# Layer 0's q, k and v from 15 block products in place of 18, in a fused two-layer attention kernel

## The chip, the cores and the metric

The kernel runs on one core of one Trainium2 chip. A core has five engines that work side by side, each through its own queue, strictly in the order in which its instructions were compiled: TensorE (PE: matrix products into PSUM), VectorE (DVE), ScalarE (ACT: activations and copies), GpSimd (POOL) and SyncE (SP, used here to issue DMA transfers). They wait for each other through semaphores. The metric is the device time of one execution in microseconds (us), smaller is better. PSUM has eight banks of 128 x 512 float32; a product of TensorE goes to one of them and has to be copied or used from there before the bank can be taken again.

## The reference, cut to what matters

The input x is 8 images of 32 x 32 positions (T = 1024) with 384 channels, float32. Layer 0 is attention with 6 heads of 64 and decomposed relative positions, after a group norm; layer 1 is causal attention with one head of 384 and, for images 0 to 4, an FFN of two products with sign-binarised weights whose results are scaled by the group's absolute maximum and clipped. Of layer 0 this is what the change concerns:

```python
qkv = x.reshape(b, hw, c) @ qkv_w + qkv_b        # (1024 x 384) @ (384 x 1152), per image
qkv = qkv.reshape(b, hw, 3, NH, HD).transpose(2, 0, 3, 1, 4)
```

In blocks of 128 channels, q transposed (3 blocks of output channels x 1024 positions) is a 3x3 block matrix of weights times a 3x2 block matrix of the image (3 blocks of channels, 2 halves of 512 positions). The plain way takes 3 x 3 x 2 = 18 block products for q, as many for k and for v.

## The kernel before, in words

The images go one after the other in the order 5, 0, 1, 2, 3, 4, 6, 7. For each: layer 0's q, k, v, the position terms, the scores and the output projection (`layer0`, `attend0_fast`), then layer 1 (`attention1`), then for images 0 to 4 the FFN (`ffn`). The group norm of the next image is made during layer 1 of the present one. A second, general path of the program stands behind a branch that this input doesn't take; the names in the profile have f_ in front of the fast path's tiles.

*q, k (L438, L466, L468).* `project_qk(b, xT, m)` makes one block of 128 output channels for both halves: three products each of 128x128x512 accumulate in a PSUM bank. m = 0 to 2 is q, 3 to 5 is k. A float32 product is two passes of TensorE, so q and k take 72 passes of 512 columns per image. ScalarE brings the first half out (with scale and bias), VectorE the second. k is stored in a permuted order of positions.

*Position terms (L484, L489, L490).* Behind the block that follows q block p, `positions(p)` multiplies q block p by the relative position table (tile rel; called rel(p) below): for each half two products in two banks. ScalarE copies one half of the rows of each bank out, VectorE the other, into the two pages called far. SP writes them to DRAM and reads them back skewed into near. `place(p, ...)` then rounds near to its high part (ScalarE, L517, twice 64x1024) and its low part (VectorE, L519), and SP and GpSimd copy these into r (L524, eight transfers each per p). The scores (L588, q times k, with L592, r times a unit pattern added into the same bank) need r.

*v (L536, L538, L539).* `values(j)` makes 128 positions x 384 channels from three products whose stationary operand is the image (every second position, `keys`) and whose moving operand is the weight, 384 columns: 8 x 3 x 2 = 48 passes. ScalarE and VectorE copy out in turn.

*Ahead of time.* Where the present image has an FFN, two blocks of the next image's q are made inside it: m = 0 between the two halves of the FFN's layer norm (`ffn`, behind the last transpose) and m = 1 between the FFN's first product y1 (L898) and its second y2 (L939). Their PSUM banks stay taken until layer 0.

*The FFN's other work.* Between y1 and y2 stand VectorE's maximum (L909, L852), GpSimd's all-reduce over partitions (L854), and the Gelus of `activate` (ScalarE L924, L925, VectorE L926), which make each block of activations as a high part hi and a low part lo. After y2 comes another maximum and all-reduce, then GpSimd clips y2 in eight pieces (L949) and VectorE adds them to x (L953), whose result GpSimd sends out (L994). These last steps (`finish`, `add`, kept in `unfinished`) are called inside the next image's layer 0, behind `positions(2)`.

The tile framework orders each engine's instructions ahead of time from its own estimates, within the order of the program and of `issue_after`, and puts in the semaphores; on the chip each engine keeps to that order. Buffers come from pools: image (11 buffers of 3 x 1024), flat (larger), page (1024 wide), small, and o_tile, the PSUM banks.

Of the kernel before, what the change touches and what calls it, by code (L numbers as in the profile page):

```python
# [37 lines left out]


# [3 lines left out]
class Pools:  # L43
    def __init__(self, ctx, tc, path):
# [5 lines left out]
        self.image_ = pool("image", 11)  # L50
# [25 lines left out]
def conv_attn_hybrid(  # L76
# [35 lines left out]
    wqkv_sb, wproj_sb, wv_sb = (tile_of(n, [P, NC, w]) for n, w in (("wqkv_sb", 3 * C), ("wproj_sb", C), ("wv_sb", C)))  # L112
    bqk, bv, b1_sb = (tile_of(n, [P, w]) for n, w in (("bqk", 6), ("bv", NC), ("b1_sb", NM)))
# [5 lines left out]
    def load_weights(pools):  # L119
# [8 lines left out]
        src = qkv_w.rearrange("(p k) o -> p k o", k=NC)  # L128
        for i in range(3):
            nc.sync.dma_start(out=wqkv_sb[:, :, ts(i, C)], in_=src[:, :, ts(i, C)])  # L130
# [5 lines left out]
        nc.scalar.mul(bqk[:, 0:NPAIR], bqk[:, 0:NPAIR], qscale)  # L136
        nc.scalar.mul(rel, rel, 1.0 / qscale)
        early = pools.small.tile([P, 1], F32, tag="early", name="early_root")
        nc.scalar.activation(early, ones[:, 0:1], AF.Sqrt)

# [70 lines left out]
    w2s = store.tile([P, NM * C], F32R, name="w2s")  # L211
    wqk = const.tile([P, NC, C], F32, name="wqk")
# [92 lines left out]
    def stages(pools):  # L305
# [125 lines left out]
        ahead = {}  # L431
# [11 lines left out]
        def layer0(b, xT):  # L443
# [5 lines left out]
            r = []  # L449
# [3 lines left out]
            def queries_keys(m):  # L453
                p = m % NPAIR
                bias = bqk[:, m : m + 1]
                made = ahead.pop((b, m)) if (b, m) in ahead else project_qk(b, xT, m)
                for half, ps in enumerate(made):
# [16 lines left out]
            def positions(p):  # L474

                if p < 1:
                    *pages, near = (pools.page(f"{n}_{b}_{p}") for n in ("far0", "far1", "near"))
                else:
                    room = pools.flat(f"far_{b}_{p}")
                    *pages, near = (room[:, ts(i, T)] for i in range(3))  # L480
                for half in range(2):
                    ps = [pools.o_tile(f"rel_{b}_{p}_{half}_{par}") for par in range(2)]
                    for par in range(2):
                        nc.tensor.matmul(  # L484
                            ps[par], rel[rows[par]].rearrange("d a n -> d (a n)"), q[rows[par], p, ts(half, 512)],
                            start=True, stop=True,
                        )
# [19 lines left out]
            def place(p, near, pages, behind=(None, None)):  # L507
# [12 lines left out]
                for part in range(4):  # L520
                    for d in range(2):
                        for i in range(2):
                            half = part % 2 if d else part // 2
                            (nc.gpsimd if i else nc.sync).dma_start(  # L524
                                out=r[part][:, p, :].bitcast(F32).rearrange("(m i) t -> i m t", i=4)[2 * i + d],
# [14 lines left out]

            near = []
            for m in range(2 * NPAIR):
                queries_keys(m)
                if 0 < m <= NPAIR:
                    near.append(positions(m - 1))
                if m == NPAIR and unfinished:
                    unfinished.pop()()

                    early = pools.small.tile([P, 1], F32, tag="early", name=f"early0_{b}")
                    nc.scalar.activation(early, k[:, 0, T - 1 :], AF.Exp, scale=0.0)  # L550
            for j in range(NJ):
                values(j)
            r.extend(pools.image(f"r_{b}_{part}", F32R) for part in range(4))
# [18 lines left out]
        def attend0_fast(residual, b, q, k, r, v, later):  # L572
# [10 lines left out]
            def scores(p, c, half):  # L583

                sc = [pools.o_tile(f"s0_{b}_{p}_{c}_{half}_{par}") for par in range(2)]
                with behind_last():
# [4 lines left out]
                    for par in range(2):  # L591
                        last_matmul[0] = nc.tensor.matmul(  # L592
                            sc[par], unit[rows[par], c // 2 % 2].rearrange("i h w -> i (h w)"),
                            r[2 * (c // 4) + c % 2][rows[par], p, ts(half, 512)], start=False, stop=True,
# [81 lines left out]
        def attend0_general(residual, b, q, k, r, v, later):  # L676
# [3 lines left out]
            def scores(u):  # L680
# [6 lines left out]
                for half in range(2):  # L687
# [3 lines left out]
                    for i in range(4):  # L691
                        nc.tensor.matmul(
                            sc[half][:, ts(i, P)], r[2 * half + i % 2][rows, p, ts(j, P)],
# [179 lines left out]
        def ffn(xt, b, gn):  # L873

            xs = [pools.halves(f"{n}_{b}", F32R) for n in ("lnT_2", "lnlo_2")]
            for half in range(2):
# [4 lines left out]
                if half == 0 and gn is not None and pools.fast:  # L881
                    with tc.issue_after(last_transpose[0]):
                        ahead[AFTER[b], 0] = project_qk(AFTER[b], gn, 0)

            early = pools.small.tile([P, 1], F32, tag="early", name=f"early_{b}")
# [27 lines left out]
            if gn is not None and pools.fast:  # L913
                ahead[AFTER[b], 1] = project_qk(AFTER[b], gn, 1)
# [3 lines left out]
            def activate(j, m0, m1):  # L918
# [131 lines left out]
```

## Time and profile before

| | us |
|---|---|
| median of 3 runs | 2351.95 (2351.21 to 2352.78) |
| the profiled execution | 2350.82 |
| its span in the profile | 2348.8 |
| TensorE busy | 2324.9 (99%), granted clock 0.999 |
| VectorE, ScalarE, GpSimd busy | 1433.9, 1041.7, 316.6 |
| q and k products (L438), 576 passes | 257.4 busy |
| v products (L536), 384 passes | 125.2 busy |
| image 1's layer 0, end of y2 to the first score | 595.36 to 637.78 |

How to read it: busy time is the sum of an engine's instructions in the execution; the share is of the span. In a table by stages each row gives a stretch, its length, then the busy time and the number of instructions of PE, PEld, DVE, ACT and POOL, the granted TensorE clock, the busy share of the DMA engines and their GB/s. PEld is TensorE's loading of its stationary operand, which overlaps its products. In a row of a group, the numbers behind the bar are its busy time and the mean of one instruction in ns, then the idle time of the engine just before it and what ended it. In rows of one line, durations are minimum/median/maximum in ns with the first and last start in us. The end of a matmul is modelled, some 0.16 us after the next one starts; the time that one takes from the stream is the distance of starts.

### The profile page before, as it was taken

What the parts mean: (1) busy time and instruction counts of PE and PEld (TensorE: products, weight loads), DVE (VectorE), ACT (ScalarE), POOL (GpSimd) and SP (SyncE); (2) the same over time, 40 slices, a digit from 0 to 9 for tenths busy, and PEclk for the clock granted to TensorE, in tenths of its full rate; (3) what the DMA queues carried; (4) which work ended last, traced back from release to release, by engine and by line L of the source; (5) the groups of instructions that cost most, each with busy time, mean ns of one, the idle gap of its engine ahead of it and who ended that gap; (6) DMA issues with size and microseconds to landing.
All of it is one profiled execution on the core that took longest, in us unless ns stands there. A gap on an engine that the chain in (4) does not pass through costs nothing.

```text
span 2348.8 us, 26174 instructions
## 1 busy us (share of the span) xinstructions
PE 2324.9 (99%) x9442; PEld 1288.2 (55%) x9442; DVE 1433.9 (61%) x2302; ACT 1041.7 (44%) x1763; POOL 316.6 (13%) x421
## 2 busy tenths in 40 slices
PE   7999999999999999999999999999999999999998
PEld 3445544568545577445684455864457744554454
DVE  3685568665587347684466864558734668525851
ACT  3551156137463256642365522747324656115621
POOL 0420013000230001310002300023000131001300
PEclk9999999999999999999999999999999999999999
DMA  6431361130631003520107211063101262017100
GB/s 166 146 117 37 104 146 38 54 135 1 144 99 68 20 21 91 118 88 14 41 12 166 65 68 41 1 138 105 68 1 41 68 139 63 1 51 146 45 1 29
DMA packets 154795, 169.99 MB, mean 72 GB/s; under 512 B 113408, under 2 KB 126048, under 8 KB 153120
## 3 DMA queue, kind: packets, MB, share of 16 engines
q1 hardware_dynamic: 134416, 98.93, 17.2%
q0 software_dynamic: 17184, 69.22, 9.7%
q8 instruction: 77, 1.26, 0.2%
q10 hardware_dynamic: 3056, 0.08, 0.1%
q14 instruction: 62, 0.51, 0.1%
HBM read 75.38 MB, written 42.47 MB: 50 GB/s over the span
## 4 chain that ended last, share of the span: by engine, by line
PE 99%; DVE 1%; DMA 0%; issue 0%; ACT 0%; DVEq 0%
PE f_s L588 14%; PE f_av L613 14%; PE f_qk L438 11%; PE f_s L775 8%; PE f_av L790 8%; PE f_y L939 7%; PE f_y L898 7%; PE f_pj L386 5%; PE f_v L386 5%; PE f_v L536 5%; PE f_q L734 5%; PE f_s L592 4%; PE f_rel L484 2%; PE f_pt L314 1%; PE f_den L631 0%; DMA f_gnT<-in_xT 0%
## 5 line engine op out<-in xcount | busy, mean ns | idle before, releaser
L598 ACT ACTIVATE f_pr<-f_s 128x512 f32<-128x512 f32 x768 | 413.6, 595 | 54.2 <-PE f_s L592 46.8
L588 PE MATMUL f_s<-f_q,f_k 64*128 64x512 f32 x1536 | 399.0, 595 | 0.0
L605 DVE TENSOR_TENSOR f_sum<-f_sum,f_pr 128x1024 f32<-128x1024 f32 x288 | 365.8, 1270 | 22.6 <-ACT f_pr L598 0.5
L613 PE MATMUL f_av<-f_pr,f_v 128*64 128x512 f32 x1536 | 339.4, 594 | 0.0
L592 PE MATMUL f_s<-f_r,unit 64*128 64x512 f32 x768 | 307.6, 792 | 0.0
L438 PE MATMUL f_qk<-f_gnT,wqkv_sb 128*128 128x512 f32 x576 | 257.4, 600 | 1.5 <-DVE f_gnT L349 1.5
L588 PEld LDWEIGHTS f_s<-f_q,f_k 64*128 64x128 f32 x1536 | 145.7, 186 | 127.4 <-issue 67.3
L613 PEld LDWEIGHTS f_av<-f_pr,f_v 128*64 128x64 f32 x1536 | 106.2, 137 | 196.3 <-issue 192.4
L775 PE MATMUL f_s<-f_q,f_lnT 128*128 128x512 f32 (+3 forms) x576 | 195.9, 488 | 0.0
L790 PE MATMUL f_av<-f_v,f_pr 128*128 128x385 f32 x576 | 195.3, 486 | 0.0
L438 PEld LDWEIGHTS f_qk<-f_gnT,wqkv_sb 128*128 128x128 f32 x576 | 108.0, 191 | 143.2 <-issue 131.5
L784 ACT ACTIVATE f_pr<-f_s 128x512 f32<-128x512 f32 (+3 forms) x96 | 47.1, 491 | 267.7 <-DVE f_s L780 220.7
L524 POOL DMA_DIRECT2D f_r<-f_far x192 | 102.2, 535 | 461.7 <-DVE f_far L519 450.9
L790 PEld LDWEIGHTS f_av<-f_v,f_pr 128*128 128x128 f32 x576 | 108.2, 190 | 77.3 <-issue 11.5
L775 PEld LDWEIGHTS f_s<-f_q,f_lnT 128*128 128x128 f32 x576 | 102.0, 190 | 77.8 <-issue 53.8
L902 ACT ACTIVATE f_h<-f_y,b_sb 128x256 f32<-128x256 f32 x240 | 100.9, 472 | 67.5 <-PE f_y L898 66.9
L909 DVE TENSOR_REDUCE am<-f_h 128x1 f32<-128x1024 f32 (+2 forms) x80 | 71.5, 946 | 96.3 <-ACT f_h L902 96.3
L734 PE MATMUL f_q<-f_lnT,wqk 128*128 128x512 f32 x288 | 127.5, 592 | 0.0
L386 PE MATMUL f_pj<-wproj_sb,f_oT 128*128 128x384 f32 x384 | 127.3, 488 | 0.0
L386 PE MATMUL f_v<-wv_sb,f_lnT 128*128 128x384 f32 x384 | 126.5, 486 | 0.0
L536 PE MATMUL f_v<-wqkv_sb,f_gnT 128*128 128x384 f32 x384 | 125.2, 486 | 0.0
L592 PEld LDWEIGHTS f_s<-f_r,unit 64*128 64x128 f32 x768 | 75.1, 187 | 90.0 <-issue 90.0
(153 smaller groups left out, 3024.9 us busy)
## 6 DMA issues: line engine op xcount, KB each, us to landing
f_far<-f_far SPq DMA_DIRECT2D x48, 512.0 KB, 3.2
f_r<-f_far POOLq DMA_DIRECT2D x192, 128.0 KB, 3.9
f_r<-f_far SPq DMA_DIRECT2D x192, 128.0 KB, 3.2
f_gnT<-in_xT SPq DMA_DIRECT2D x24, 512.0 KB, 4.6
f_x<-in_x SPq DMA_DIRECT2D x32, 384.0 KB, 7.5
out_y<-f_x POOLq DMA_DIRECT2D x28, 384.0 KB, 4.4
f_far<-f_far SPq DMA_DIRECT2D x128, 64.0 KB, 4.9
f_w1a<-w1s POOLq DMA_DIRECT2D x5, 1536.0 KB, 7.0
```

Source lines behind the costliest of these rows:

```text
L386: nc.tensor.matmul(ps[:, :C], xT[:, k, ts(j, P)], w[:, k, cols], start=(k == 0), stop=(k == NC - 1))
L438: nc.tensor.matmul(made[half], wqkv_sb[:, i, ts(m, P)], xT[:, i, ts(half, 512)], start=(i == 0), stop=(i == NC - 1))
L536: nc.tensor.matmul(ps, keys[:, i, j // 2, j % 2], wqkv_sb[:, i, 2 * C :], start=(i == 0), stop=(i == NC - 1))
L588: nc.tensor.matmul(sc[par], k[rows[par], p, ts(c, P)], q[rows[par], p, ts(half, 512)], start=True, stop=False)
L592: last_matmul[0] = nc.tensor.matmul(sc[par], unit[rows[par], c // 2 % 2].rearrange("i h w -> i (h w)"), r[2 * (c // 4) + c % 2][rows[par], ...
L598: last_exp[0] = nc.scalar.activation(pr[:, ts(par, 512)], sc[par], AF.Exp).ins
L605: adds.append(nc.vector.tensor_tensor(total, total, pr, ALU.add).ins)
L613: last_matmul[0] = nc.tensor.matmul(av[ts(par, HD), :], v[:, c, ts(2 * p + par, HD)], pr[:, ts(par, 512)], start=(c == 0), stop=(c == NJ - 1),
L734: nc.tensor.matmul(ps, wqk[:, k, ts(m, P)], xT[:, half, k, :], start=(k == 0), stop=(k == NC - 1))
L775: nc.tensor.matmul(sc[:, lo:], xT[:, c // 4, k, ts(c % 4, P)], q[:, half, k, lo:], start=(k == 0), stop=(k == NC - 1),)
L790: nc.tensor.matmul(av[:, : C + 1], prs[c][:, ts(j - c, P)], v[:, c, :], start=(c == 0), stop=(c == j))
L898: nc.tensor.matmul(ps, w1k[i // 2][:, ts(m, P)], xs[i % 2][:, half, i // 2, :], start=(i == 0), stop=(i == 2 * NC - 1))
```

## The change

q, k and v (three sets) are each made from 15 products in place of 18. A product is a sum of weight blocks times a sum of image blocks. The six blocks of a result are sums of the products in groups, so that the products are collected in six PSUM banks, A to F. B and A collect eleven of them as running sums: after most of their products ScalarE copies the bank's present value out (`keep`), and the next product goes on in the same bank. Four times per set GpSimd subtracts one such copy from another; at the end VectorE brings each bank out, adding or subtracting a kept sum (`put_queries`, `put_keys`, `put_values`). Below, "A5" is product number 5 in bank A; "n6", "m7" are names of kept sums.

- The weight sums (`weight_forms`) are made once at the start: GpSimd for q, VectorE for k and v. For v the products are 4 x (128 x 128 x 128): the moving operand is a weight block of 128 columns.
- The image sums (`image_forms`), eleven operations of 128x512, are made by VectorE for image 5 and by GpSimd, during the layer 1 before, for the others.
- Ahead of time, six q products are made in the layer-norm gap, five between y1 and y2, and the twelfth (B3) is issued within y2; three are left to layer 0. k's products are laid around the three `positions(p)`, two before each, and `finish` is called behind `positions(0)`; TensorE's order of all these is fixed (`in_turn`). The Exp table's early load moves behind k.
- Memory: one image buffer less (10); r takes three flats shared by pairs of p; far and near of p = 0 and the FFN's hi and lo move to flats; the FFN writes x to DRAM in the layer norm and reads it back during y2 (`spilt`, `xagain`).

```diff
+PROD_ORDER = (
+    ("A", 5, "m5"), ("B", 11, "m11"), ("A", 13, "n0"), ("B", 6, "n1"), ("A", 12, "n2"), ("B", 0, "n4"),
+    ("A", 4, "n3"), ("B", 1, "n5"), ("A", 10, "n6"), ("D", 8, None), ("C", 7, "m7"),
+    ("B", 3, None), ("F", 9, None), ("A", 2, None), ("E", 14, None),
+)
+PROD_FIRST = tuple(PROD_ORDER[i] for i in (9, 12, 14, 0, 1, 2, 3, 4, 5, 6, 7, 8, 10, 11, 13))
+PROD_COMBINE = {"n1": ("n0", "n1"), "n2": ("n2", "m11"), "m7": ("m7", "n3"), "n6": ("n5", "n6")}
...
+    def weight_forms(pools, eng, raw, s):
+        add(s1, w(0, 1), w(0, 2))
+        add(f(8), w(0, 0), s1)
+        add(s2, w(2, 0), w(2, 2))
+        add(f(9), w(2, 1), s2)
...
+        def image_forms(b, xT, eng):
+            sub(5, x(2, 1), x(0, 1))
+            sub(5, f[5], x(1, 1))
+            add(2, x(2, 0), x(2, 1))
+            sub(0, f[2], x(1, 0))
+            sub(1, x(1, 1), f[0])
+            add(11, f[1], x(0, 1))
+            sub(4, x(0, 0), f[2])
+            add(7, f[4], x(0, 1))
+            add(13, f[7], x(1, 1))
+            sub(6, x(1, 0), x(2, 0))
+            sub(12, x(2, 0), x(0, 0))
...
+            def multiply(self, ps, r, start):
+                x, w = self.forms[r], wf[:, r, self.s, :]
+                if self.s < 2:
+                    in_turn(ps, w, x, start=start, stop=True, skip_group_check=True)
+                    return
+                keys = x.rearrange("p (g i n) -> p g n i", g=2, n=2)
+                for j in range(4):
+                    in_turn(
+                        ps[:, ts(j, P)], keys[:, j // 2, j % 2], w, start=start and j == 0, stop=True, skip_group_check=True
+                    )
+            def keep(self, ps, name):
+                dst = self.kept(name)
+                if self.s == 2:
+                    nc.scalar.copy(dst, ps)
+                    return
...
+                nc.scalar.activation(dst, ps, AF.Identity, bias=bias, scale=scale)
+            def run(self, n, final=None):
+                for self.now in range(self.at, self.at + n):
+                    bank, r, name = self.order[self.now]
...
+                    self.multiply(self.banks[bank], r, start)
+                    if name is not None:
+                        self.keep(self.banks[bank], name)
+                    if name in PROD_COMBINE:
+                        dst, other = PROD_COMBINE[name]
+                        nc.gpsimd.tensor_tensor(self.part[dst], self.part[dst], self.part[other], ALU.subtract)
...
-                if p < 1:
-                    *pages, near = (pools.page(f"{n}_{b}_{p}") for n in ("far0", "far1", "near"))
-                else:
-                    room = pools.flat(f"far_{b}_{p}")
-                    *pages, near = (room[:, ts(i, T)] for i in range(3))
+                room = pools.flat(f"far_{b}_{p}")
+                *pages, near = (room[:, ts(i, T)] for i in range(3))
...
+            def put_queries(ps, kept, p, half, op):
+                nc.vector.scalar_tensor_tensor(q[:, p, ts(half, 512)], ps, qscale, kept, ALU.mult, op)
+            def put_keys(ps, kept, p, half, op):
+                dst = k[:, p, ts(half, 512)].rearrange("d (g n i) -> d g i n", n=2, i=P)
+                ps, kept = (t.rearrange("d (g i n) -> d g i n", n=2, i=P) for t in (ps, kept))
+                nc.vector.tensor_tensor(dst, ps, kept, op)
+            def put_values(ps, kept, p, half, op):
+                ps, kept = (t.rearrange("t (j c) -> t j c", j=4) for t in (ps, kept))
+                nc.vector.tensor_tensor(v[:, 4 * half : 4 * half + 4, ts(p, P)], ps, kept, op)
+            def products():
+                forms = xf.pop(b)
+                of_q = ahead.pop(b, None) or ProductSet(b, 0, forms, PROD_FIRST)
+                of_q.run(N_PROD - of_q.at, put_queries)
+                of_k, of_v = (ProductSet(b, s, forms) for s in (1, 2))
+                for p in range(NPAIR):
+                    of_k.run(2, put_keys)
+                    near.append(positions(p))
+                    if p == 0 and unfinished:
+                        unfinished.pop()()
+                of_k.run(N_PROD - of_k.at)
+                early = pools.small.tile([P, 1], F32, tag="early", name=f"early0_{b}")
+                nc.scalar.activation(early, k[:, 0, T - 1 :], AF.Exp, scale=0.0)
+                of_v.run(N_PROD, put_values)
...
-                        ahead[AFTER[b], 0] = project_qk(AFTER[b], gn, 0)
+                    ahead[AFTER[b]] = ProductSet(AFTER[b], 0, xf[AFTER[b]])
+                    last_product[0] = last_transpose[0]
+                    ahead[AFTER[b]].run(6)
+            nc.sync.dma_start(out=spilt, in_=xt.rearrange("p j c -> p (j c)"))
...
-                ahead[AFTER[b], 1] = project_qk(AFTER[b], gn, 1)
+                ahead[AFTER[b]].run(5)
...
+                room = pools.flat(f"hilo_{b}_{j}", F32R)[:, : 3 * T].rearrange("p (i m q) -> p i m q", i=2, q=P)
...
+                if j == 4:
+                    xt = pools.flat(f"xagain_{b}")[:, : NJ * C].rearrange("p (j c) -> p j c", j=NJ)
+                    nc.sync.dma_start(out=xt.rearrange("p j c -> p (j c)"), in_=spilt)
...
+                raw = load_weights(pools)
+                weight_forms(pools, nc.gpsimd, raw[0], 0)
...
+                xf[ORDER[0]] = image_forms(ORDER[0], gn, nc.vector)
+                weight_forms(pools, nc.vector, raw[1], 1)
+                weight_forms(pools, nc.vector, raw[2], 2)
...
+                            xf[AFTER[b]] = image_forms(AFTER[b], made, nc.gpsimd)
```

## The prediction

> **What bounds the kernel now.** I read the busy shares and the chain that ended last first, then the groups that the change touches.
>
> ```profile
> PE 2324.9 (99%) x9442; PEld 1288.2 (55%) x9442; DVE 1433.9 (61%) x2302; ACT 1041.7 (44%) x1763; POOL 316.6 (13%) x421
> PE 99%; DVE 1%; DMA 0%; issue 0%; ACT 0%; DVEq 0%
> L438 PE MATMUL f_qk<-f_gnT,wqkv_sb 128*128 128x512 f32 x576 | 257.4, 600 | 1.5 <-DVE f_gnT L349 1.5
> L536 PE MATMUL f_v<-wqkv_sb,f_gnT 128*128 128x384 f32 x384 | 125.2, 486 | 0.0
> ```
>
> TensorE is the whole chain, so a pass saved is worth its pace and a new wait of TensorE its full length. Next, an image whose predecessor had an FFN (images 1, 2, 3, 4 and 6): busy time by stage around image 0's FFN, and the chain through image 1's layer 0, piece by piece (start, length).
>
> ```profile
> 516.25:522.70 6.45, 6.45 (x26) 3.52 (x24) 4.01 (x14) 3.74 (x7) 0.00 (x0) 1.00 0.00 0
> 556.00:561.30 5.30, 5.30 (x14) 2.43 (x13) 2.98 (x9) 2.90 (x6) 0.38 (x1) 1.00 0.00 0
> 595.20:622.10 26.90, 26.90 (x73) 11.13 (x73) 18.91 (x32) 12.38 (x19) 10.06 (x14) 1.00 0.70 190
> ...
> 597.27 5.35 PE f_qk L438 x12
> 602.62 1.92 PE f_rel L484 x8
> 604.54 5.35 PE f_qk L438 x12
> 609.89 1.92 PE f_rel L484 x8
> 611.80 10.50 PE f_qk L438 x24
> 622.30 15.48 PE f_v L536 x48
> 637.78 1.06 PE f_s L588 x4
> ```
>
> The first two stages are the layer-norm gap and the gap between the FFN's products: TensorE is full there too, because twelve q passes of the next image fill each, and the granted clock is 1.00. Layer 0 runs from 595.36 to 637.78 without a gap. Last, the rows of what will stand beside it: the FFN's clip on GpSimd, position transfers and casts, and six 128-column passes in a row.
>
> ```profile
> L949 POOL TENSOR_SCALAR f_y<-f_y,qu,ql x40: 646/655/1327, 604.1 to 1872.1; 128x384 f32<-128x384 f32 x40
> L949 POOLq MODIFY_POOL_CONFIG  x10: 83/83/83, 597.1 to 1859.7; - x10
>   PE f_rel L484: 34.9, 5
> DMA to landing us min/median/max: 2.4/3.9/9.4
> L517 ACT CAST f_far<-f_near x16: 1050/1522/1997, 46.7 to 2132.8; 64x1024 fp32r<-64x1024 f32 x16
> 255.13:255.80 0.67, 0.67 (x6) 0.64 (x5) 1.00 0.00 0
> ```
>
> After the all-reduce GpSimd takes 34.9 / 5 = 7.0 us to its first clip, put down to a matmul long done; a MODIFY_POOL_CONFIG stands in its queue there. The DMA line is GpSimd's r transfers.
>
> **What is saved.** A 512-column pass takes 0.429 us (pass starts 519.257 and 519.686), a product two. q and k: 72 - 60 = 12 passes fewer, 5.15 us per image. v: 48 passes in 15.48 us become 15 x 4 x 2 = 120 passes of 128 columns. Six took 0.67, so 0.1115 each: 13.4 us, 2.1 saved. Bounds: a third of a 384-column pass (15.48 / 48 / 3 = 0.1075: 12.9 us) and weight loads one after the other at 196 ns (the row of v's loads: 23.5 us, a loss of 8). I take 0.1115, the same form, whose loads of 192 ns already overlap. Together 7.25 us per image, 58.0 for eight. [...]
>
> **Hand-over of A and B.** (A5 is product 5 in bank A.) The next product on A waits for ScalarE's copy: 1.04 (start to end of a product's result) + 0.69 (L468) + 0.16 (signal and load) = 1.89 against 1.72 for two products, 0.17 per pair. q has four pairs: 0.7. k mostly has the rel products between: 0.2 to 0.35. v's copies take 0.59: 0.2.
>
> **Layer-norm gap (five times).** Six products in place of twelve passes, the same 5.15 us, but two copies of 0.69 now stand in ScalarE before the 1.283 us table load of L363, and the next copy behind it. Old load: 518.56; now the second product's copy ends at 518.86, load and root end 520.35, the copy of the third product 521.04, so its bank is free at 521.2, when TensorE would have had four products done at 519.9. The remaining two end at 522.9 instead of 521.4: **+1.5** (0.5 to 2.3, by how much of 1.28 + 0.69 is seen).
>
> **Between y1 and y2 (five times).** Five products (4.29 us) replace twelve passes; B3 moves into y2. ScalarE has two more copies between the Gelus of j = 0 (after hi0 and after hi1). hi0 still ends 559.79, then copy 0.69, Gelu, hi1 ends 561.6, copy 0.69, Gelu, hi2. TensorE waits 0.7 for hi1, 0.6 for the third lo, 0.6 for the first lo of j = 1 (the two hi now stand before the two Gelus), 0.1 before: **+2.0** (1.0 to 3.0). GpSimd's new combine waits for another 7 us return after the all-reduce, but its reader is at j = 6.
>
> **The clip (five times).** In the changed kernel's order VectorE runs: four copies of rel(0), all eight adds (each waits for its clip), then the copies of rel(1), and behind them every end of k. The second half of rel(2) needs the banks of rel(1). With t = 0 at the end of y2: F's end and the maximum 2.0, all-reduce 2.5, first clip 2.5 + 6.9 = 9.4, eight clips in 6.1 us (604.09 to 610.20), last add 16.2, two copies of 0.69: 17.6. TensorE is there after nine products (7.7), two and a half rel (4.8) and 0.35: 12.9. **+4.7.** Before, adds and copies alternated and the k products filled the time. Bounds: 3.5 if the clips start at 8.8 as before, 6.2 with slower clips (to 1.327).
>
> **The position cast in v (seven times).** ScalarE's first L517 cast (1.05 to 2.0, 1.53 mean) stands before the copy that A10 waits for. That has 0.7 of slack beside B1: **+1.2** (0.3 to 2.0).
>
> **The r transfers (eight times).** VectorE's second cast (L519, 1.2 to 1.96) now stands behind the end of A, last but one; before, it ran at 626.80, 11 us before v's end. With v's end as zero: A's matmuls end -0.9, the sum on VectorE 0.0, cast 1.5, GpSimd issue 1.6, landing +3.8: 5.4. The first score's r product is due at 1.0: **+4.4** (landing 2.7: 3.3; 5.8: 6.4), 2.4 at image 5, where the bias products take 2.0. SP's parts of the same rows wait for ScalarE's second cast, which stands behind C's copy: -2.8, cast -1.3, landing 3.2 later, so they come before GpSimd's. Behind the stalled r product stand all scores; queued behind it on GpSimd are only the later parts, 0.53 each against 1.09 per score step. r(2) reuses pair 0's room, but pair 1 lies between.
>
> **Start-up, image 5.** VectorE makes the sums from 15.7: eleven of 0.69, then 44 weight sums at 0.29 (L780's row) before q's ends. A5 waits to 18.3, B11 to 21, k's rel(0) to about 37-40, so v ends about **2.2** us later than the old 68.7 instead of 7 earlier (0 to 6).
>
> **Hidden at nothing.** GpSimd's eleven image sums (1.28 each, up to 2.85: 14 to 31 us from 478) stand before the w1a issue; with 7.0 to land it is there by 500 to 517, y1 starts 522.7. Spill and reload of x have 30 us and come before the adds; uncovered, 7 us per FFN. The flats of hi/lo return one step (4.2 us) before they are needed.
>
> **Sum.** Five FFN followers: -7.25 + 0.2 + 0.2 + 1.5 + 2.0 + 4.7 + 1.2 + 4.4 = +6.95, 34.8. Images 0 and 7: -7.25 + 1.25 + 1.2 + 4.4 = -0.4 each. Image 5: +4.6. Total +38.6 on the profiled execution's 2350.8 (span 2348.8 and 2.0 around it): 2389.4. The median 2351.95 stands 1.1 higher: **2390**.
> [...]
>
> **Rivals.**
> *VectorE's order does not reach TensorE.* Place: the second half of rel(2) and the first r product. For it: VectorE is only 61% busy and ran far ahead before. Against: both orders are fixed and both chains are made of measured lengths. Price 23.5 + 33.2 = 56.7 less: 2333. It decides (faster than before) once these two cost under 18 of the 56.7.
> *v's short passes become load-bound* at 196 ns: 10.1 us per image, 81 more: 2471. For it: keys are loaded with a stride, never in short passes. Against: loads of 192 ns paced 111.5.
> *GpSimd and VectorE slow each other.* A GpSimd sum of 128x512 took 1.28 alone and up to 2.85; two late combines and the cast slower by 1.5 each before the r transfers: some 3 per image, 24 more: 2414.
> *The products are not saved*: the compiled order has 15 q, 15 k and 60 v matmuls, so hardly; it would be 58 more: 2448.
>
> **How the numbers follow.** Main sum 0.72, VectorE's order harmless 0.14, load-bound 0.04, GpSimd 0.08, not saved 0.02. All low ends together give 2349, all high ends 2438, neither likely; the main case's own range is 2360 to 2415. For 8 in 10: 2352 to 2425; left out are most of the first rival and the two dearest. 0.2% (4.7 us) is what a measurement tells from no change: faster 0.12, same 0.04, slower 0.84.
>
> **What will show it.** 480 passes of 512 and 960 of 128 columns, the latter at 0.11 us; TensorE's busy share falling to about 95%; TensorE idle about 4.7 at rel(2) waiting for VectorE's copies, and 4.4 before each image's first r product, waiting for a GpSimd transfer; the layer-norm gap 8.0 instead of 6.45. Wrong if r lands before v's end, if the second cast runs early, or if the v stage is not near 15 us.

## The result, and the profile after

The changed kernel takes 2442.29 us (median of 4 runs, 2438.29 to 2443.08) against 2351.98 before: 1.0381 times as long, interval 1.0363 to 1.0399. It is slower, as predicted, but by 90 us in place of 38, outside the predicted range. The profiled execution took 2442.92 us with a span of 2441.2, so the two spans differ by 92.4.

Of the page after, the busy times, the chain that ended last, and the group of the r products:

```profile
PE 2326.3 (95%) x9922; PEld 1321.1 (54%) x9922; DVE 1518.5 (62%) x2419; ACT 1123.2 (46%) x1927; POOL 552.8 (23%) x615
PE 84%; DVE 5%; DMA 4%; ACT 2%; POOL 2%; SPq 2%; issue 1%; ACTq 0%; DVEq 0%
L793 PE MATMUL f_s<-f_r,unit 64*128 64x512 f32 x768 | 314.4, 809 | 38.9 <-DMA f_r<-f_far 35.5
```

Before, TensorE was 99% busy and was 99% of the chain. Now every other engine has a share of it. But TensorE's busy time is not less, though products were saved: 2324.9 before, 2326.3 after. That is the first sign that something makes its work longer. The waits of TensorE after (total us, times, longest):

```profile
PE f_s L793 <- DMA f_r<-f_far: 35.5, 10, 5.4
PE f_rel L500 <- DVE f_far L663: 28.8, 5, 6.3
PE f_y L1144 <- DVE f_hilo L1127: 6.8, 5, 1.7
...
PE f_s L793 <- issue: 3.3, 1, 3.3
```

The first two rows are the two long waits of the prediction: the first r product of each image behind the r transfers, and the second half of rel(2) behind VectorE's copies, once per image that follows an FFN. The third is early in y2, 7.5 us behind its start in image 0's FFN. The last is image 5's first r product, whose transfers come late too. Now both places of image 1 by stages (stretch, length, then busy time of PE, PEld, DVE, ACT and POOL, granted clock, DMA share, GB/s):

```profile
625.00:630.00 5.00, 5.00 (x17) 1.78 (x17) 3.06 (x6) 4.20 (x9) 2.80 (x4) 1.00 0.60 221
630.00:633.00 3.00, 0.84 (x4) 0.01 (x2) 1.80 (x4) 1.57 (x3) 3.00 (x4) 1.00 1.22 95
633.00:636.00 3.00, 0.00 (x0) 0.00 (x0) 2.17 (x4) 0.00 (x0) 2.99 (x4) 0.67 1.49 61
636.00:641.00 5.00, 4.67 (x7) 2.02 (x8) 4.53 (x8) 1.16 (x2) 4.44 (x5) 0.52 0.94 332
641.00:646.00 5.00, 5.00 (x12) 2.02 (x12) 1.68 (x2) 3.25 (x5) 1.90 (x2) 1.00 1.06 333
663.00:668.00 5.00, 1.18 (x8) 0.48 (x6) 2.08 (x2) 0.00 (x0) 2.62 (x5) 1.00 0.89 189
668.00:675.00 7.00, 5.29 (x20) 2.25 (x16) 1.23 (x1) 3.00 (x6) 0.00 (x0) 0.51 0.51 141
```

TensorE stops at 630.84. At 634.0, 3.2 us later, its granted clock falls to half (0.50); work resumes at 636.33 and runs at half clock until 640.8. In 636 to 641 it issues 7 instructions in 4.67 us, in the next stretch of the same length 12. The wait for r, 663.7 to 667.5, is followed in the same way by 6.8 us at half clock. The whole trace has 14 such stretches, 95.6 us in all, 70.9 of them with work, each 3.4, 6.8 or 10.2 us long. Their starts and ends all lie on one grid with a step of 3.413 us, which runs through the whole trace. So the time from a stop to the fall of the clock is not fixed: behind the twelve waits of over 3.8 us it was 2.1 to 4.9 us. The prediction's rows showed a granted clock of 1.00 everywhere, and it charged a wait its length alone.

From the traces I worked out, for each kernel, the time between TensorE's first and last matmul in which it does nothing (idle), the work lost in stretches of half clock (taken as half the busy time there), and what is left, its work at full clock:

| kernel | span | idle | lost at half clock | work at full clock |
|---|---|---|---|---|
| before | 2348.8 | 4.5 | 0 | 2324.9 |
| after | 2441.2 | 96.2 | 35.4 | 2290.8 |

So the +92.4 are, but for rounding, 91.8 (idle) + 35.4 (half clock) - 34.1 (work) - 0.8 (start and end). In the chain of image 1 a product of q and k takes the 0.86 us that was forecast, at half clock 1.97, and a product of v 0.94 in place of 0.892. The lower lines are a second, shorter wait for r behind the first one: an issue on SP's queue, its transfer of 5.73, and then the r product that needs it:

```profile
639.01 1.97 PE f_pr_A L500 x2
640.98 0.86 PE f_pr_B L500 x2
...
648.94 0.94 PE f_pr_B L500 x8
...
664.84 0.50 SPq L697
665.38 5.73 DMA f_r<-f_far
671.24 0.79 PE f_s L793 x2
```

### The profile page after: what moved, and what is told of

The parts are those of the page before. It is cut to its first block, busy times and chain, and to the rows that moved or that the text cites. A ratio compares the mean times of both kernels' runs of the same rounds, so it can differ in the third digit from the quotient of the medians.

```text
span 2441.2 us, 27862 instructions
## 1 busy us (share of the span) xinstructions
PE 2326.3 (95%) x9922; PEld 1321.1 (54%) x9922; DVE 1518.5 (62%) x2419; ACT 1123.2 (46%) x1927; POOL 552.8 (23%) x615
## 4 chain that ended last, share of the span: by engine, by line
PE 84%; DVE 5%; DMA 4%; ACT 2%; POOL 2%; SPq 2%; issue 1%; ACTq 0%; DVEq 0%
PE f_s L789 14%; PE f_av L814 13%; PE f_av L991 7%; PE f_s L976 7%; PE f_y L1102 7%; PE f_y L1144 6%; PE f_pj L450 5%; PE f_v L450 5%; PE f_q L935 5%; PE f_s L793 4%; PE f_pr_A L500 3%; PE f_pr_B L500 2%; DMA f_far<-f_far 2%; DMA f_r<-f_far 1%; PE f_rel L500 1%; PE f_pt L378 1%
## 5 line engine op out<-in xcount | busy, mean ns | idle before, releaser
L789 PE MATMUL f_s<-f_q,f_k 64*128 64x512 f32 x1536 | 414.6, 616 | 0.0
L793 PE MATMUL f_s<-f_r,unit 64*128 64x512 f32 x768 | 314.4, 809 | 38.9 <-DMA f_r<-f_far 35.5
L789 PEld LDWEIGHTS f_s<-f_q,f_k 64*128 64x128 f32 x1536 | 152.3, 193 | 125.5 <-issue 66.0
L581 POOL TENSOR_TENSOR f_u_n<-f_u_n,f_u_n 128x512 f32<-128x512 f32 x96 | 122.7, 1288 | 269.4 <-ACT f_u_n L566 160.5
L804 DVE TENSOR_TENSOR f_sum<-f_pr,f_pr 128x1024 f32<-128x1024 f32 x48 | 69.0, 1438 | 133.8 <-ACT f_pr L799 133.8
L511 POOL TENSOR_TENSOR f_xf<-f_gnT 128x512 f32<-128x512 f32 x28 | 35.8, 1291 | 503.0 <-DVE f_gnT L413 503.0
L976 PEld LDWEIGHTS f_s<-f_q,f_lnT 128*128 128x128 f32 x576 | 102.0, 190 | 77.8 <-issue 53.8
L1144 PE MATMUL f_y<-f_w2a,f_hilo 128*128 128x384 f32 x640 | 132.3, 345 | 9.0 <-DVE f_hilo L1127 6.8
```

The lines of the kernel that those rows point to most:

```text
L789: nc.tensor.matmul(sc[par], k[rows[par], p, ts(c, P)], q[rows[par], p, ts(half, 512)], start=True, stop=False)
L793: last_matmul[0] = nc.tensor.matmul(sc[par], unit[rows[par], c // 2 % 2].rearrange("i h w -> i (h w)"), r(2 * (c // 4) + c % 2, p)[rows[pa ...
L976: nc.tensor.matmul(sc[:, lo:], xT[:, c // 4, k, ts(c % 4, P)], q[:, half, k, lo:], start=(k == 0), stop=(k == NC - 1),)
L1144: nc.tensor.matmul(ps[:, :C], h, w, start=(i == 0), stop=(i == len(products) - 1))
```

## The experiments

Three questions: are the two long waits what they were said to be; is half clock their second price; and was the time lost to order alone, or would 15 products not pay even without waits? Theories are named in each expectation.

**Each of the two waits alone.** The first kernel moves VectorE's eight adds of the clipped result behind the last copy of rel(2):

```diff
-                        nc.vector.tensor_copy(
+                        last_far[0] = nc.vector.tensor_copy(
...
-                    if p == 0 and unfinished:
-                        unfinished.pop()()
+                    if p == 2 and unfinished:
+                        unfinished.pop()(last_far[0])
```

> The changed kernel, but the FFN's closing step is called behind the third position product and its eight adds stand behind all position copies on VectorE, so that rel(2) does not wait for GpSimd's clip. In the changed kernel five waits there cost TensorE 28.9 us (5.5, 5.8, 5.4, 5.9, 6.3) and behind each of them the granted clock is 0.50 for 6.9 to 10.3 us. Theory A (a wait costs its length, and then the matmuls that run at half clock behind it): 29 us and 2 to 3.5 more each time, some 42 less, 2400. Theory B (the low clock costs nothing, what comes after is late for other reasons, transfers and slow VectorE): only the waits, 29 less, 2413. Theory C (no loss there that something else would not cause again): no change, 2442.

Measured: 2398.76 (ratio 1.0201, 1.018 to 1.0221), 43.5 less than after and within 1.3 of the 2400. The row of rel is gone from the waits, the one of r is as it was:

```profile
PE f_s L793 <- DMA f_r<-f_far: 36.4, 12, 5.4
```

Idle fell by 29.8 and the work lost at half clock by 10.7 (35.4 to 24.7). The wait cost more than its length, and the rest of it was clock.

The second kernel issues the casts and transfers of pair 0 ahead of v's products, and v's copies, sums and image combines behind them:

```diff
+                with self.after(0):
+                    nc.scalar.copy(dst, ps)
...
+                of_v.behind = place(0, *near[0])
                 of_v.run(N_PROD, put_values)
...
-            place(0, *near[0])
+                place(0, *near[0])
```

> The changed kernel, but the first position block is cast and sent before v's copies, sums and ends on ScalarE, GpSimd and VectorE, as far as each queue goes. In the changed kernel the first r products wait 3.3 to 5.4 us in each of the eight images, with a second wait of 1.7 in one, 37.7 in all, a copy in v waits some 1.2 behind the cast, and the clock is at 0.50 for 3.4 to 10.3 us afterwards. Theory A: 37.7 and 8 x 1 of the cast and some 20 at half clock: 65 less, 2377. Theory B: 46 less, 2396. Theory C: the cast earlier in v delays v as much as it gains: 2435 or more.

Measured: 2421.93 (1.0299, 1.0279 to 1.032); A had 2377 and B 2396, and only 20 us went. The waits say why:

```profile
PE f_rel L500 <- DVE f_far L670: 27.5, 5, 5.9
PE f_pr_A L500 <- ACT f_u_m L565: 12.5, 8, 1.8
PE f_s L799 <- ACT f_pr L809: 9.3, 16, 0.7
```

The r row is gone; in its place stand two that the edit brought. v's first copy waits behind ScalarE's casts (12.5 in all). And the score pairs 1 and 2 each got the PSUM bank of the pair before them, so that TensorE waits for exponentials (row three and longer passes: the first 30 passes of the scores take 7.75 us in place of 5.55 before, 2.2 per image); in the changed kernel pair 1 takes banks that v has left. The trace does not name the bank; that it was shared is argued from these waits, and they are gone in the kernel ordered by hand below. So the transfers' lateness is what stalls r, but this order pays for it elsewhere.

**Both together.** Both edits in one kernel.

> Both edits together. Theory A: all clock episodes but that at the start go, 105 less, 2337, below the kernel before (2352). Theory B: 75 less, 2367, still slower than before. Theory C: 2430 or more.

Measured: 2392.88 (1.017, 1.0152 to 1.0189): none of the values given. The chain through image 1 (start, length, what) shows two new waits:

```profile
629.15 3.19 DVE f_xagain L1168 x7
633.28 1.11 DVE f_k L729
634.41 0.21 ACT early L750
635.70 2.00 ACT f_far L698
637.72 0.59 ACT f_u_m L565
638.36 1.97 PE f_pr_A L500 x8
...
652.40 1.06 PE f_s L799 x4
653.73 0.59 ACT f_pr L809
654.37 1.12 PE f_s L799 x2
```

The adds (f_xagain) now delay k's last sum, on which the Exp table's load waits (early); behind that stand ScalarE's casts and v's first copy, and TensorE waits 3 to 4 us at v in the images that follow an FFN. Its first v product then takes 1.97 in place of the 0.94 of the later ones, the length that the changed kernel's trace gave at half clock to a product of q and k. The lower lines are the shared bank: exponential, product, exponential.

**Fill the wait in place of removing it.** The changed kernel, but the first q times k pair is made six times (the same values in the same bank), so that TensorE works while r is on its way:

```diff
-                    for par in range(2):
-                        nc.tensor.matmul(
-                            sc[par], k[rows[par], p, ts(c, P)], q[rows[par], p, ts(half, 512)], start=True, stop=False
-                        )
+                    again = 5 if (p, c, half) == (0, 0, 0) else 0
+                    for i in range(again + 1):
+                        for par in range(2):
+                            nc.tensor.matmul(
+                                sc[par], k[rows[par], p, ts(c, P)], q[rows[par], p, ts(half, 512)], start=True, stop=i < again
+                            )
```

> The changed kernel with every wait as it is, but in each image the first pair of q times k products is made six times over (the same result, some 4.3 us of work) before the first r product, so that TensorE is busy while it waits for r. Theory A: the wait is as long but the clock stays at 1.00, and the eight first score stages (17 to 25 us, 20.5 us in all above those of the kernel before) lose 10 to 17 of that: 2425 to 2432. Theory B: no gain: 2442 or slightly more.

Measured: 2434.36 (1.0352, 1.0331 to 1.0373), 8 less with 34 us more work (the filler is inside the former wait).

```profile
PE f_rel L500 <- DVE f_far L663: 28.3, 5, 6.1
PE f_s L795 <- DMA f_r<-f_far: 5.6, 6, 1.9
```

The row of r is down to 5.6 and the work lost at half clock from 35.4 to 20.2. The time lies nearer to A than to B, but its interval touches that of after, so this run leans to A and doesn't settle it.

**The price of a wait by itself.** The kernel *before*, whose idle time is 4.5 us in all, with one wait per image put between v and the first score: a chain of ScalarE copies on a spare page, and a small product of TensorE that needs it. Two lengths: five copies of the spare page, shown here, and one.

```diff
+            idle = pools.page(f"idle_{b}")
+            nc.gpsimd.memset(idle, 0.0)
+            nc.scalar.copy(idle[:, :C], v[:, NJ - 1, :])
+            for _ in range(5):
+                nc.scalar.copy(idle, idle)
+            none = pools.o_tile(f"none_{b}")
+            last_matmul[0] = nc.tensor.matmul(none[:, :16], idle[:, :P], idle[:, :16], start=True, stop=True).ins
```

> The same with four more copies in the chain, a wait of about 6 us. Theory A (a wait costs its length, and over some 3 us half a clock for the first microseconds of work behind it as well): 2352 + 8 x (6.0 + 2.0) = 2416 (2408 to 2424), and eight stretches of 3.4 to 6.9 us at clock 0.50. Theory B (a wait costs its length): 2400 (2396 to 2406).

> The kernel before, with one wait for TensorE added in each image between v and the first score: a tiny product that needs a chain of ScalarE copies of v's last block, about 2.3 us long. Both theories: under 3 us the clock does not fall, so the time grows by the wait alone, 8 x 2.3 = 18 us: 2370 (2366 to 2376), and no stretch at half clock.

The longer: 2422.22 (1.0296, 1.0275 to 1.0317), +70.1 on the 2352.15 of the runs beside it, where A had 2416 and B 2400. The wait's row, then image 1's wait by stages:

```profile
PE f_none L585 <- ACT f_idle L583: 51.1, 8, 6.6
```

```profile
650.00:655.00 5.00, 5.00 (x16) 2.75 (x14) 0.56 (x1) 0.48 (x1) 0.00 (x0) 1.00 1.04 197
655.00:658.40 3.40, 0.05 (x1) 0.00 (x0) 0.56 (x1) 2.60 (x3) 0.00 (x0) 1.00 0.51 143
658.40:661.60 3.20, 0.00 (x0) 0.00 (x0) 0.00 (x0) 3.11 (x3) 0.00 (x0) 0.51 0.00 0
661.60:665.30 3.70, 3.63 (x10) 2.02 (x12) 0.00 (x0) 0.57 (x3) 0.00 (x0) 0.50 0.00 0
665.30:670.00 4.70, 4.70 (x30) 2.47 (x26) 2.48 (x3) 4.33 (x10) 0.00 (x0) 1.00 0.02 3
```

The clock is half from 3.4 us after TensorE stopped, for 6.8 us; the last 3.6 of them fall on work (fourth row, PE busy 3.63 at a granted clock of 0.50). All eight waits (seven of 6.6 and image 5's of 4.7) are followed by 6.8 us at half clock: 51.1 of waiting and 16.3 of lost work make 67.4 of the measured +70.1. Nothing of the change is in this kernel, so the second price belongs to the wait.

The shorter: 2376.93 (1.0104, 1.0083 to 1.0124), +24.8; 2370 was expected, with no half clock. The waits add up to 16.9 (2.6 at most), and three of the eight, each of 2.3 us, were followed by one stretch of 3.4 us at half clock. The one of 2.6 was not. Image 1's wait and the stretch at half clock behind it, then the time right behind the wait of 2.6:

```profile
644.70:647.00 2.30, 0.00 (x0) 0.00 (x0) 0.56 (x1) 1.56 (x2) 0.00 (x0) 1.00 0.62 191
648.60:652.10 3.50, 3.50 (x14) 1.55 (x10) 0.23 (x1) 2.17 (x4) 0.00 (x0) 0.51 0.00 0
967.20:971.00 3.80, 3.77 (x22) 2.18 (x24) 0.00 (x0) 2.04 (x4) 0.00 (x0) 1.00 0.01 2
```

At half clock TensorE does 14 instructions of the scores in 3.5 us, at full clock 22 in 3.8. 16.9 and 5.1 of lost work make 22.0 of the +24.8. The 2.8 and 2.7 us left in the two kernels are near what TensorE's work at full clock grew by in the traces (3.9 and 3.1), where the added product and the modelled ends ahead of the waits count. The stretches of 3.4 and 6.8 us have lengths that the changed kernel's trace shows too. In that trace none of the waits under 2 us was followed by half clock and each of the 14 of 3.3 us and more was; the limit of 3 us in the expectation lay between these groups. Here three waits of 2.3 us were hit and the one of 2.6 was not. What decides which of them are hit is not shown.

**Is the order all that was wrong?** The order around layer 0 is set by hand, with the same products: adds behind the last copy of rel(2); pair 0's casts before the Exp table's load; its transfers before the round trips of pairs 1 and 2 on SP's queue; the combines of v after GpSimd's transfers or before them as each is needed; the first exponentials behind v's last sum, so that pair 1 takes v's banks.

```diff
+                casts(*near[0])
                 early = pools.small.tile([P, 1], F32, tag="early", name=f"early0_{b}")
-                nc.scalar.activation(early, k[:, 0, T - 1 :], AF.Exp, scale=0.0)
-                of_v.run(N_PROD, put_values)
+                with tc.issue_after(marks[0]):
+                    nc.scalar.activation(early, k[:, 0, T - 1 :], AF.Exp, scale=0.0)
+                of_v.behind = marks
+                of_v.run(5)
+                transfers(0, near[0][1], last_combine[0])
+                for p in (1, 2):
+                    with tc.issue_after(marks[2]):
+                        trips(p)
+                of_v.run(N_PROD - of_v.at, put_values)
...
+                with tc.issue_after(last_value[0]):
+                    for par in range(2):
+                        last_exp[0] = nc.scalar.activation(pr[:, ts(par, 512)], sc[par], AF.Exp).ins
```

> Both waits removed again, with what held the run with both edits back taken away too: layer 0's casts of the first pair go ahead of the Exp table load on ScalarE, their transfers go ahead of the position trips of pairs 1 and 2 on SP's queue, and the first scores' exponentials are ordered behind v's last sum, so that the second and third score pairs take v's banks and not the bank of the pair before them. Theory A (waits, plus half the clock after each long one): of the 2393 us with both edits, 8 x 2.6 = 21 us were the score pairs that waited for each other's exponentials on one bank, and 5 x (3.1 + 1.8) = 24 us were v's start behind the Exp table load; without them 2348, 2335 to 2365. Rival D (the products themselves are dearer than counted, and their sums slow the other engines, so no order of the work brings it back): above 2380.

Measured: 2348.81 (10 runs; 0.9991, 0.9981 to 1.0) on an expectation of 2348. The whole loss is gone with the same products:

```profile
PE 2292.7 (98%) x9922; PEld 1311.3 (56%) x9922; DVE 1529.4 (65%) x2419; ACT 1115.4 (48%) x1927; POOL 577.8 (25%) x615
```

Idle is 33.4, lost at half clock 5.1, work at full clock 2287.6. The two stages in the FFN are still as long as in the changed kernel: 1.5 and 2.1 us more than before, five times over, 18.

**Which part makes r late?** The changed kernel with v from its eight plain blocks, q and k from 15 products:

```diff
-                of_k, of_v = (ProductSet(b, s, forms) for s in (1, 2))
+                of_k = ProductSet(b, 1, forms)
...
-                of_v.run(N_PROD, put_values)
+                for j in range(NJ):
+                    values(j)
```

> v by its eight blocks of the kernel before, q and k by 15 products as after; nothing is reordered. Theory A (the wait for r is ScalarE's and GpSimd's work for v's products ahead of r's casts and transfers): the wait ahead of the first r product goes, with the half clock after it: 8 x (5.0 + 2 + 0.5) = 60 us less, v's own passes 8 x 1.4 = 11 us more, 2393 (2380 to 2410). Rival E (r is late because of VectorE's sums for k and SP's queue, which stay as they are): the wait only shrinks by the 1.4 us that v is longer, 2440 (2430 to 2450).

Measured: 2428.78 (1.0326, 1.0305 to 1.0346), nearer to E, though just outside the range of either. (VectorE's sums of v's weights fall away too, and image 5's v begins 4.2 us earlier.)

```profile
PE f_rel L503 <- DVE f_far L666: 27.6, 5, 6.0
PE f_s L799 <- DMA f_r<-f_far: 12.3, 8, 2.0
PE f_s L799 <- issue: 12.2, 7, 2.2
```

The two rows of the r products together (DMA and issue) are down from 38.8 to 24.5, and the wait at rel(2) stays. But v also takes longer here (15.57 us per image against 14.75): 6.6 of the 14.3 would come from that alone if the transfers kept their time. So v's form is one cause of the late r transfers, and not the larger. What else is in it, VectorE's sums and adds or the transfers queued on SP, no run tells apart.

**The stages in the FFN too.** The next kernel is the one ordered by hand, and also takes the q products ahead of time in another order (D8 and F9 between products of A and B, so that a copy has two more products to end in) and two of ScalarE's copies behind the Gelus of j = 0.

```diff
+PROD_AHEAD = tuple(PROD_ORDER[i] for i in (0, 1, 9, 12, 2, 3, 4, 5, 14, 6, 10, 7, 8, 11, 13))
...
-                    ahead[AFTER[b]] = ProductSet(AFTER[b], 0, xf[AFTER[b]])
+                    ahead[AFTER[b]] = ProductSet(AFTER[b], 0, xf[AFTER[b]], PROD_AHEAD)
...
-                ahead[AFTER[b]].run(5)
+                ahead[AFTER[b]].run(5, held=("n3", "m7"))
```

> The run above, and in the layer norm's gap q's products that need no copy out of PSUM (D8, F9) stand between the first two and the next two; two copies out of PSUM wait behind the GELUs of the first y2 tile. Theory A: the 1.5 us at the layer norm and the 2.0 us between y1 and y2 were ScalarE's order of copies and table loads and GELUs, so 5 x (1.4 + 1.6) = 15 us less than the run above, 2333, and below the kernel before (2352). Rival D: the same time as the run above within 4 us, since the gaps come from the products' own sums.

Measured: 2381.42 (1.0123, 1.0106 to 1.0139), 48 more than expected. In the timeline (start, length, engine, line, instruction, and in brackets the idle time ahead), GpSimd's combine now stands right ahead of the all-reduce, which begins 5.75 us after GpSimd came free, and y2 behind it waits 5.31:

```profile
890.12 1.26 POOL L582 TENSOR_TENSOR f_u_n<-f_u_n,f_u_n 128x512 f32<-128x512 f32 x1 [35.02 <-ACT f_u_n L571]
897.14 0.38 POOL L1101 PARTITION_ALL_REDUCE qa<-qg  x1 [5.75 <-issue]
898.93 4.85 PE L1193 MATMUL f_y<-f_w2a,f_hilo 128*128 128x384 f32 x14 [5.31 <-ACT f_hilo L1172]
```

The all-reduce waits for nothing that the profile shows. In the kernel before, GpSimd's queue has a MODIFY_POOL_CONFIG for the all-reduces (10, of 49 ns) as for the clips (10, of 83 ns), and the way back, from an all-reduce to the first clip, took 7.0 us. I read the 5.75 us as the price of GpSimd's change from ordinary operations to the all-reduce; what happens in them is not shown. Five such waits (27.3 in all) and the half clock behind them (11.4, of 18.2 lost in the whole execution) are most of the miss. The mended kernel issues these two combines behind the all-reduce, takes q's last combine to VectorE, and puts the first two copies of the layer-norm gap behind the casts there:

```diff
-                self.combine("m7")
+                for name in self.later:
+                    with tc.issue_after(last_reduce[0] or behind):
+                        self.combine(name)
...
-                    ahead[AFTER[b]].run(6)
+                    ahead[AFTER[b]].run(6, held=("n0", "n1"))
```

> The run all_free again, with two slips of it mended: the combine of n2 stands behind the all-reduce on GpSimd's queue (in all_free it stood right ahead of it, and the all-reduce then began 5.75 us late, once an image), q's combine for n6 is VectorE's, and the two copies out of PSUM in the layer norm's gap stand behind the casts of the layer norm. Theory A, as for all_free: the layer norm's gap and the gap between y1 and y2 are ScalarE's order, 5 x (1.4 + 1.6) = 15 us less than no_waits: 2334 (2326 to 2342). Rival D: within 4 us of no_waits.

Measured: 2337.46 (0.994, 0.9924 to 0.9957): 0.4 to 0.8% faster than before, so that it beats both kernels. It is 11.4 below the kernel ordered by hand; 15 had been expected. The layer-norm gap is back to within 0.4 us of before, but between y1's end and y2's end 1.4 of the 2.1 us stay. The wait in y2 is down to 1.7 in all:

```profile
PE f_y L1200 <- DVE f_hilo L1181: 1.7, 5, 0.4
```

The accounts of all kernels, as above:

| kernel | span | idle | lost at half clock | work at full clock |
|---|---|---|---|---|
| adds behind rel(2) | 2399.7 | 66.4 | 24.7 | 2289.5 |
| r early | 2418.3 | 77.7 | 21.3 | 2300.7 |
| both | 2392.1 | 59.4 | 17.1 | 2296.9 |
| wait for r filled | 2429.0 | 64.7 | 20.2 | 2324.6 (with filler) |
| v plain | 2424.2 | 76.9 | 29.4 | 2299.0 |
| order by hand | 2344.9 | 33.4 | 5.1 | 2287.6 |
| FFN stages too, first form | 2379.4 | 59.8 | 18.2 | 2282.9 |
| FFN stages too, mended | 2333.8 | 23.5 | 6.0 | 2285.1 |

## Why the prediction was right in direction and wrong in size

*The step that failed* is in "What bounds the kernel now": that a new wait of TensorE is worth "its full length". The eight waits of 4.7 to 6.6 us put into the kernel before cost their length and 2.0 us of work each at half clock behind them (16.3 / 8), and here such stretches took 35.4 us of the 53.8 by which the sum fell short (92.4 against 38.6). No row of before could show it, since before had no such wait; the clock column stood at 1.00 throughout, and its falling should have been a rival with a price.

*The term that was mis-sized* is "What is saved". It had 58.0, less 5.7 of the hand-overs of A and B, which lengthen passes and are not seen as gaps: 52.3. TensorE's work at full clock fell by 34.1. The largest part of the 18.2 between, 7.0, is v's: its products saved 8.3 (124.5 to 116.2, from the distances of starts at full clock) and not 15.2. Of these 7.0, 15 x 8 x (0.94 - 0.892) = 5.8 are the pace: its passes of 128 columns take 117.5 ns each, where the row of six in before gave 111.5. The products of q and k saved 35.3, 1.8 short of their 37.1. The rest is on products that the change left as they were: rel 3.5, y2 3.2 and the scores 2.4 longer. Why is not shown; a product right ahead of a wait counts to its modelled end, which is part of it. 5.7 came back in the mended kernel (2290.8 against 2285.1).

*The waits were right*: 90.9 predicted without the hand-overs, 91.8 found. That the sum is so close is in part luck: the clip and the r transfers cost 5.3 and 5.6 us more than forecast, the position casts 6.7 less. By its parts:
- Layer-norm gap: from the end of layer 1's last product with v to the start of y1, 6.2 became 7.7; +1.5 predicted and found.
- Between y1 and y2: from y1's end to y2's end 39.1 became 41.1 to 41.8 (mean 41.4); +2.0 predicted, 2.3 found.
- The clip: +4.7 predicted, 5.8 found (28.8 / 5). The clips started 9.4 after y2's end (627.20 against 617.8), as worked out from GpSimd's 7.0, but eight took 7.7 and not 6.1 (each add runs beside the next clip). The chain through image 2 is the one that was worked out: eight clips, the last add behind them, VectorE's copy, and then rel goes on:

```profile
957.68 7.71 POOL f_y L1154 x8
...
966.06 0.71 DVE f_far L663
...
966.81 2.67 PE f_rel L500 x4
```

Where the adds were moved behind rel(2), the eight clips had VectorE's copies beside them in place of the adds, and took 5.14:

```profile
623.24 5.14 POOL L1154 TENSOR_SCALAR f_y<-f_y,qu,ql 128x384 f32<-128x384 f32 x8 [6.70 <-DVE f_far L663]
```

- The position cast in v: +1.2 predicted, 0.2 found. The cast took 1.04, and the slack beside B1 hid the rest. With the longer passes v's stage takes 14.75 us, and the forecast's parts give 14.8 (13.4 + 0.2 + 1.2): two errors that cancel.
- The r transfers: +4.4 predicted, 4.85 found (38.8 / 8). SP's parts do not always come before GpSimd's, as the prediction had it: image 1 waits 1.7 of its share for one of them (7.00 - 5.29 in the last stretch above).
- Start-up: v's end in image 5 was forecast 2.2 us later than before and came 5.0 later (73.89 against 68.89), 1.7 of it work lost at half clock behind a wait of 3.5 at the first rel.

*The rivals.* VectorE's order was not harmless: the two waits are there, each in its place. v is not load-bound: 0.94 a product, not 1.57. GpSimd was slowed, but at the clips: eight took 7.7 us beside VectorE's adds and 5.14 beside its copies. The wait for r came out only 0.45 above its term. The products are saved: 9922 passes with 480 of 512 columns in q and k. One sign came true by luck: TensorE's busy share fell to 95% as forecast, but of busy time that had not shrunk (2326.3), 35.4 of it lost at half clock.

## What to carry to other kernels

In these kernels, where TensorE was the chain and had hardly rested (4.5 us before), the new waits cost about a third more than their length, in work at half clock behind them (5.1 on 16.9 and 16.3 on 51.1 where waits were put in, 35.4 on 96.2 in the changed kernel): put such a price into the sum. When work is moved in such a kernel, its followers move too: look at which PSUM bank the next products get, what stands behind the moved instruction on each queue, and what kind of operation GpSimd did just before (5.75 us ahead of an all-reduce here). Fewer products did pay here, 0.6%, but only with the queues' order set for them; as the change was made they cost 3.8%.

## What the runs showed of the hardware that was not expected

In the changed kernel the granted clock fell to half 2.1 to 4.9 us after TensorE stopped, behind each of its 14 waits of 3.3 to 6.3 us, and stayed there for 3.4, 6.8 or 10.2 us, also when work had resumed; all falls and returns of this trace lie on one grid of 3.413 us. Of the eight shorter waits put into the kernel before (16.9 us in all, 2.6 the longest) three were followed by 3.4 us at half clock, of the eight longer ones (4.7 to 6.6 each) all, by 6.8 us. GpSimd's all-reduce began 5.75 us after an ordinary operation that ended right ahead of it, where the engine waited for nothing that the profile shows; TensorE's five waits behind it were 27.3 us in all. And eight clips on GpSimd took 7.7 us with an add of VectorE beside each, 5.14 with VectorE's copies beside them in place of the adds.
